# A two-layer attention kernel on one core: query tiles scaled one by one, copies moved to VectorE, and a few steps of the first attention moved

## The chip, the cores and the metric

The kernel runs on one core of a Trainium2 chip, in one launch. The metric is the device time of the launch in microseconds (us). The engines are PE (TensorE's matmuls), PEld (its weight loads, which overlap the matmuls), DVE (VectorE), ACT (ScalarE), POOL (GpSimd) and SP (SyncE, which issues DMAs). All data are float32.

## The reference, cut to what matters

Eight sequences of 256 tokens with 256 features go through two layers. Each layer is a cross-attention to a context of 192 features, followed by a feed-forward block; both have a residual sum.

```
x = x + attention0(layernorm(x), ctx)      # 16 heads of 16
x = x + soft_moe(x)                        # 8 experts, 128 slots each per sample, hidden 1024
x = x + attention1(layernorm(x), ctx)      # 16 heads of 64, with an output bias
x = x + channel_mix(layernorm(x))

attention:  q = x Wq, k = ctx Wk, v = ctx Wv, split into heads
            out = softmax(q k^T * head_dim**-0.5) v Wo      # the first with a key mask
soft_moe:   logits of tokens against slots (both normalised)
            combine = softmax over slots, dispatch = softmax over tokens
            slots = dispatch^T x -> two-layer expert with gelu -> combine
```

The soft mixture of experts works on groups of two sequences here, so its routing needs, for each group, a softmax over slots for each token and a softmax over tokens for each slot.

## The kernel before, in words

**Stages.** Four stages follow one another: the first attention (0 to about 259 us of the profiled span), the mixture of experts (259 to 895), the second attention (895 to 1269) and the channel mix (1269 to the end). The routing of the first group of the mixture of experts is laid into the last steps of the first attention, so that PE has work there.

**Order.** `matmul` and `transpose` (L74, L77) keep PE's instructions in the order in which the program issues them. `vec` and `gps` do the same for VectorE and GpSimd while `Ordered.held` is set, which it is through the loop of the first attention (L103 is the line of their instructions). Elsewhere a scheduler may reorder the other engines' instructions. Semaphore waits come out of the data: an instruction waits for whatever wrote what it reads, and for whatever still reads what it overwrites.

**PSUM.** Three kinds of buffer are used: "big" (128x1024, two banks, 2 buffers), "mm" (128x512, one bank, 3 buffers, `ps_mm`) and "o" (128x512, one bank, 1 buffer, `ps_o`). A "mm" buffer is taken in turn by every projection, transpose and logit piece, so its third successor waits until its reader is done.

**First attention.** The loop at L907 runs over steps `h` of about 3 us; eight steps serve one sequence. A step issues eight score matmuls for queries and eight for the exponentials' side (`scores`, ACT's exponentials are `ex` at L585), then whatever `whole[h]` lists: small pieces put there by `at(h, piece)`. A piece may return a function, its second half, which is called in the next step, after that step's scores. Pieces that the change touches are:

- `normed0(b)` (L680): the layer-normed input of sequence `b`, `xh`, written by GpSimd for the later sequences.
- `values0(b)` (L708 and L709): V of a sequence, in two halves. The first half issues two matmuls and returns the second, which issues the others and copies V out of PSUM.
- `slot_scaled(e2)` and `slot_piece(e2)` (L412): the slot embeddings of two experts are scaled by GpSimd (`sn`), transposed by PE (`pt_sn`) and scaled out of PSUM by two VectorE instructions into `snT`.
- `values(b, t2, to)`: the attention's product with V for half of the heads of a sequence (PE `o <- ex,V`), its transposes and division, ten steps after the scores. It returns `turn_back`, a VectorE transpose for the next step. `turn_back` is called ahead of the halves, in one step behind them.
- `routing0(b)`: the routing of one sequence of the first group. Its pieces are N (`scale`), P (`prepare`), T (`by_token`, logits `ln`), S (`by_slot`, the transposed logits `ls`, with their maxima, exponentials and sums), U (`turn_token`, PE's `ptn` transposes, copied into `CT`), D (`turn_slot`, PE's `pts` transposes, copied into `dt`, which is the buffer `wq` in the profile) and F (`fill`, PE's `pf`, the slots). They are laid out by hand in two strings at L891: a letter, the step, and the piece's arguments.

**Second attention.** After a prologue for the first sequence, the tick loop at L1605 runs over ticks `n` of about 10.3 us, four to a sequence, each with two pairs of heads. In program order a tick has: the values of tick n-3 (`values`, PE's `o`, then its copy `ot` at L1414), one query piece for the next sequence (`q_piece`, L1296), the projection of tick n-4 (only for the last tick of a sequence, PE's `po`), the transposes of tick n-2 (`transposes`, PE's `pe`, copied into `et` at L1395 by VectorE and ACT in turn), the normalisation of tick n-1 (GpSimd), one piece of keys or values of a later sequence, and the scores of tick n (PE's `sc`, VectorE's maxima `nm` at L1361, ACT's exponentials `ex` at L1366).

A query piece covers two tiles of 128 query features by 256 tokens. Both lie in one "mm" buffer, that is in one bank:

```
pq = ps_mm(f"q1_{b}_{t2}").rearrange("p (t n) -> p t n", t=2)
for i in range(2):          # two tiles, two matmuls each
    ...matmul(pq[:, i, :], ...)
nc.vector.tensor_scalar(
    to["QT"][:, 2 * t2 : 2 * t2 + 2, :], pq, HD1**-0.5, None, ALU.mult
)
```

There are 32 query pieces, four in the prologue and 28 in ticks. In three of four ticks the transposes come straight after the query piece on PE; in the fourth the projection lies between.

Of the kernel before, what the change touches and what calls it, by code (L numbers as in the profile page):

```python
# [12 lines left out]
ALU = mybir.AluOpType  # L13
# [3 lines left out]
B, S, D, C = 8, 256, 256, 192  # L17
NT = B * S // P
H = 16
HD0, HD1 = 16, 64  # L20
# [43 lines left out]
def kernel(ctx: ExitStack, tc: tile.TileContext, a: dict, out: bass.AP):  # L64
    nc = tc.nc
# [42 lines left out]
    vec, gps = Ordered(nc.vector), Ordered(nc.gpsimd)  # L108
# [175 lines left out]
    with ExitStack() as l0:  # L284
# [126 lines left out]

        def slot_piece(e2):  # L412
            pt = transposed(sns[e2], f"sn_{e2}", transpose)
            for c in range(2):
                vec.tensor_scalar(
                    snT[:, c, e2 * 256 : (e2 + 1) * 256],
                    pt[:, c, :],
                    sgam[:, c : c + 1],
                    None,
                    ALU.mult,  # L420
                )

# [10 lines left out]
        tos = []  # L435
# [228 lines left out]
        def at(h, f):  # L664
            whole.setdefault(h, []).append(f)
# [9 lines left out]
        for p, when in ((1, (1, 2, 2, 3, 3)), (2, (5, 7, 8, 9, 11)), (3, (17, 19, 21, 23, 27))):  # L675
            parts, got = ln_parts(p, f"l0_{2 * p}")
            stats0 += [got] * 2
            for h, part in zip(when, parts):
                at(h, part)
        for b, h in ((2, 4), (3, 6), (4, 15), (5, 23), (6, 31), (7, 39)):  # L680
            at(h, lambda b=b: normed0(b))
        at(0, lambda: keys0(0, 1))
        at(1, lambda: queries0(0, 1))
# [12 lines left out]
        for p in range(1, 4):  # L696
            h, b = 16 * (p - 1), 2 * p
            if h:
                at(h, lambda b=b: tokens0(b))
                at(h + 3, lambda p=p: key_rows(p))  # L700
                at(h + 4, lambda p=p: keys0(p, 0))
                at(h + 5, lambda b=b: queries0(b, 0))
                at(h + 7, lambda b=b: queries0(b, 1))
                at(h + 8, lambda b=b: tokens0(b + 1))
                at(h + 12, lambda p=p: keys0(p, 1))
            at(h + 13, lambda b=b: queries0(b + 1, 0))
            at(h + 15, lambda b=b: queries0(b + 1, 1))
            at(h + 17, lambda b=b: values0(b))  # L708
            at(h + 25, lambda b=b: values0(b + 1))  # L709

        for e in range(E):
            at(7 + e, lambda e=e: slot_sum(e))
        at(19, slot_scale)
        for e2 in range(4):
            at((23, 31, 39, 43)[e2], lambda e2=e2: slot_scaled(e2))
            at((25, 33, 41, 45)[e2], lambda e2=e2: slot_piece(e2))
        for g, when in enumerate(((29, 31, 37, 39), (47, 49, 53, 61), (61, 64, 65, 66))):
            for i, h in enumerate(when):
                at(h, lambda g=g, i=i: moe_mean(g, [i]))
# [21 lines left out]
        def routing0(b):  # L741
# [58 lines left out]
            def turn_token(t):  # L800
                for m in range(2):
                    pt = ps_mm(f"ptn_{b}_{t}_{m}")
                    for i in range(4):
                        e = 4 * m + i
                        transpose(
                            pt[:, i * P : (i + 1) * P], st[f"en{t}"][:, e * P : (e + 1) * P]
                        )
                    (vec.tensor_copy if m else nc.scalar.copy)(
                        set0["CT"][:, b, 4 * m : 4 * m + 4, t * P : (t + 1) * P],
                        pt.rearrange("p (e n) -> p e n", e=4),  # L810
                    )
# [48 lines left out]
            def turn_slot(q):  # L860
                for t in range(2):
                    pt = ps_mm(f"pts_{b}_{q}_{t}")
                    for i in range(4):
                        transpose(
                            pt[:, i * P : (i + 1) * P],
                            st[f"es{q}"][:, i, t * P : (t + 1) * P],
                        )
                    (vec.tensor_copy if b and t else nc.scalar.copy)(dt[:, t, :], pt)

            def fill(q, c):  # L870
                pf = ps_mm(f"pf_{b}_{q}_{c}")
# [18 lines left out]
        for b, plan in enumerate(  # L890
            (  # L891
                "N43 P47 T48.00 T49.10 S50.00 S51.01 T52.01 T53.11 D54.0 U55.0 U55.1 F56.00 F57.01 "
                "S58.10 S59.11 D62.1 F63.10 F65.11",
                "N55 P60 T61.00 T64.10 S65.00 S66.01 T67.01 T68.11 D69.0 U69.0 S70.10 S70.11 U70.1 "
                "F71.00 F72.01 D73.1 F73.10 F74.11",
            )
        ):
            does = dict(zip("NPTUSDF", routing0(b)))
            for step in plan.split():
                when, _, args = step[1:].partition(".")  # L900
                at(int(when), lambda f=does[step[0]], args=args: f(*map(int, args)))
# [4 lines left out]
        for h in range(8 * B + 12):  # L906
            q, k = [  # L907
                (i // 8, i % 8 // 2, i % 2) if 0 <= i < 8 * B else None for i in (h, h - 6)
            ]
            if q or k:  # L910
                scores(q, k)

            late = turn_back if h == 8 * B + 7 else None
            if turn_back and not late:
                turn_back()
            later = [g for g in [f() for f in halves] if g]
            if late:
                late()
            turn_back = None
            k = h - 4  # L920
            if k % 4 == 0 and 0 <= k < 8 * B:
                pair_maxima(k // 8, k % 8 // 4, tos[k // 8])
            halves = later + [g for g in [f() for f in whole.get(h, ())] if g]
            k = h - 10
            if k % 4 == 0 and 0 <= k < 8 * B:
                turn_back = values(k // 8, k % 8 // 4, tos[k // 8])
        Ordered.held = False

# [272 lines left out]
    with ExitStack() as l1:  # L1201
# [61 lines left out]
        def proj1(b):  # L1263

            to = {}

            def normed_piece():
                mv, rstd = xat_stats[b // 2]  # L1270
                to["xh"] = normed(b, mv, rstd, "l1", of=4)

            def xt_piece():
                pt = transposed(to["xh"], f"x1_{b}", transpose)
                to["xT"] = p1.tile([P, 2, S], F32, tag="xT", bufs=1, name=f"xT1_{b}")
                nc.vector.tensor_copy(to["xT"], pt)  # L1276
                for t in range(2):
                    nc.gpsimd.tensor_tensor(
                        x_sb[:, 2 * b + t, :], x_sb[:, 2 * b + t, :], bo, ALU.add
                    )  # L1280

            def q_piece(t2):
                if t2 == 0:
                    to["QT"] = p1.tile([P, 8, S], F32, tag="QT", bufs=2, name=f"QT1_{b}")
                pq = ps_mm(f"q1_{b}_{t2}").rearrange("p (t n) -> p t n", t=2)
                for i in range(2):
                    t = 2 * t2 + i
                    for c in range(2):
                        matmul(
                            pq[:, i, :],  # L1290
                            lhsT=wq[:, c, t * P : (t + 1) * P],
                            rhs=to["xT"][:, c, :],
                            start=(c == 0),
                            stop=(c == 1),
                        )
                nc.vector.tensor_scalar(  # L1296
                    to["QT"][:, 2 * t2 : 2 * t2 + 2, :], pq, HD1**-0.5, None, ALU.mult
                )

            def values_of(u):  # L1300

                if u == 0:
                    to["V"] = p1.tile([P, 2, DA], F32, tag="V", bufs=2, name=f"V1_{b}")
                pv = [ps_mm(f"v1_{b}_{u}_{h}") for h in range(2)]
                t0 = S * b + u * P
                cols = [slice(h * 512, (h + 1) * 512) for h in range(2)]
                for h in range(2):
                    matmul(
                        pv[h],
                        lhsT=ctx0T[:, t0 : t0 + P],  # L1310
                        rhs=wv[:, 0, cols[h]],
                        start=True,
                        stop=False,
                    )

                def halves():
                    for h in range(2):
                        r = slice(64 * h, 64 * h + 64)
                        matmul(
                            pv[h],  # L1320
                            lhsT=ctx1T[r, t0 : t0 + P],
                            rhs=wv[r, 1, cols[h]],
                            start=False,
                            stop=True,
                        )
                    nc.scalar.copy(to["V"][:, u, cols[0]], pv[0])
                    nc.vector.tensor_copy(to["V"][:, u, cols[1]], pv[1])

                return halves

            return (
                to,
                [lambda t=t: q_piece(t) for t in range(4)],
                [lambda u=u: values_of(u) for u in range(2)],
                normed_piece,
                xt_piece,
            )

        def steps1(b, to):
# [4 lines left out]
            for t in range(8):  # L1344
# [53 lines left out]
                def values(t=t, tag=tag, st=st):  # L1398
# [12 lines left out]
                                stop=(c == 1),  # L1411
                            )
                    if t % 2 == 1:
                        nc.scalar.copy(blk["ot"][:, t - 1 : t + 1, :], blk["o"])  # L1414

                def project(tag=tag):
                    po = ps_mm(f"po_{tag}").rearrange("p (q d) -> p q d", q=2)
# [288 lines left out]
```

## Time and profile before

| what | value |
| --- | --- |
| time, median of 3 runs | 1332.44 us (1332.26 to 1334.61) |
| the profiled execution | 1334.6 us, its span 1332.8 us |
| mean granted TensorE clock | 0.997 |
| PE busy | 1315.3 us, 99% of the span |
| VectorE busy | 567.7 us, 43% |
| ACT busy | 576.6 us, 43% |
| GpSimd busy | 245.1 us, 18% |

Times in the profile are of one execution. A float32 matmul is recorded as two matmuls, so that a query piece of four matmuls shows eight. A line of the timeline gives the start, the time from the first start to the last end of what is grouped in it, the engine, the line, the operation with its output and inputs, the tile sizes and the number of instructions; the bracket gives the idle time of the engine before it and what ended that. A row of the windows gives, for a stretch of the span, its length, the busy time (and the number of instructions) of PE, PEld, DVE, ACT and POOL, the granted clock of TensorE as a share of full speed, the share of the DMA engines and GB/s. A row of the groups gives the busy time and the mean duration in ns, then the idle time of the engine before the group and what ended it.

### The profile page before, as it was taken

What the parts mean: (1) busy time and instruction counts of PE and PEld (TensorE: products, weight loads), DVE (VectorE), ACT (ScalarE), POOL (GpSimd) and SP (SyncE); (2) the same over time, 40 slices, a digit from 0 to 9 for tenths busy, and PEclk for the clock granted to TensorE, in tenths of its full rate; (3) what the DMA queues carried; (4) which work ended last, traced back from release to release, by engine and by line L of the source; (5) the groups of instructions that cost most, each with busy time, mean ns of one, the idle gap of its engine ahead of it and who ended that gap; (6) DMA issues with size and microseconds to landing.
All of it is one profiled execution on the core that took longest, in us unless ns stands there. A gap on an engine that the chain in (4) does not pass through costs nothing.

```text
span 1332.8 us, 19111 instructions
## 1 busy us (share of the span) xinstructions
PE 1315.3 (99%) x7520; PEld 955.6 (72%) x7520; DVE 567.7 (43%) x1131; ACT 576.6 (43%) x1396; POOL 245.1 (18%) x285
## 2 busy tenths in 40 slices
PE   9999999999999999999999999999999999999998
PEld 5666655577778786788867888866676676677777
DVE  6677777433320233322333110024544544544675
ACT  2644455353522363423634122213545445445653
POOL 3222412200000010100101000012323323333423
PEclk9999999899999999999999999999999999999999
DMA  7100000134134232342323434350000000000001
GB/s 218 65 1 2 1 1 1 63 103 134 68 134 134 70 132 78 124 134 72 130 82 120 134 118 151 103 154 1 0 1 1 1 1 1 1 1 1 1 8 56
DMA packets 59145, 86.85 MB, mean 65 GB/s; under 512 B 3376, under 2 KB 49072, under 8 KB 59056
## 3 DMA queue, kind: packets, MB, share of 16 engines
q1 hardware_dynamic: 58480, 85.11, 19.5%
q8 instruction: 59, 0.97, 0.3%
q10 hardware_dynamic: 576, 0.52, 0.1%
q14 instruction: 30, 0.25, 0.1%
HBM read 83.53 MB, written 2.10 MB: 64 GB/s over the span
## 4 chain that ended last, share of the span: by engine, by line
PE 94%; ACT 4%; DVE 2%; issue 0%; POOL 0%; ACTq 0%; DVEq 0%; POOLq 0%
PE ph L1104 17%; PE pe L1120 16%; PE sc L74 9%; PE q L74 7%; PE o L74 7%; PE po L74 5%; PE k L74 5%; PE pe L77 4%; PE v L74 4%; PE pc L1146 4%; PE pf L1050 3%; PE ln L968 3%; PE pf L74 1%; PE pk L74 1%; PE pr L74 1%; PE ln L74 1%
## 5 line engine op out<-in xcount | busy, mean ns | idle before, releaser
L1112 ACT ACTIVATE ht<-ph,b 128x256 f32<-128x256 f32 x256 | 119.3, 474 | 371.6 <-PE ph L1104 371.2
L1104 PE MATMUL ph<-slots,w 128*128 128x256 f32 x1024 | 266.9, 384 | 0.9 <-ACT ht L1112 0.2
L1120 PE MATMUL pe<-w,ht 128*128 128x256 f32 x1024 | 263.3, 381 | 0.0
L1104 PEld LDWEIGHTS ph<-slots,w 128*128 128x128 f32 x1024 | 182.3, 189 | 54.0 <-ACT ht L1112 21.7
L1120 PEld LDWEIGHTS pe<-w,ht 128*128 128x128 f32 x1024 | 192.0, 190 | 29.9 <-DVE slots L1129 4.2
L1379 POOL TENSOR_TENSOR ex<-ex,rz 128x1024 f32<-128x1024 f32 x64 | 119.9, 1895 | 229.9 <-DVE rz L1377 222.4
L1366 ACT ACTIVATE ex<-sc,nm 128x256 f32<-128x256 f32 x256 | 117.4, 484 | 53.0 <-DVE nm L1361 53.0
L585 ACT ACTIVATE ex<-sc 128x512 f32<-128x512 f32 x128 | 75.1, 598 | 68.7 <-PE sc L74 64.9
L74 PE MATMUL sc<-KT,QT 17*128 17x256 f32 (+1 forms) x1024 | 103.5, 380 | 0.8 <-ACT QT L520 0.7
L1028 POOL TENSOR_TENSOR es<-es,zs 128x1024 f32<-128x1024 f32 x12 | 22.7, 1894 | 432.8 <-DVE zs L1027 432.8
L103 DVE TENSOR_REDUCE NM<-sc 128x2 f32<-128x512 f32 x128 | 87.6, 691 | 32.7 <-PE sc L74 27.6
L1129 DVE TENSOR_TENSOR slots<-pe,b 128x512 f32<-128x512 f32 x32 | 22.1, 692 | 185.1 <-PE pe L1120 185.1
L74 PE MATMUL q<-xT,wq 128*128 128x256 f32 x384 | 94.9, 391 | 0.9 <-DVE xT L1276 0.9
L74 PEld LDWEIGHTS sc<-KT,QT 17*128 17x128 f32 (+1 forms) x1024 | 75.9, 186 | 20.8 <-issue 11.6
L74 PEld LDWEIGHTS q<-xT,wq 128*128 128x128 f32 x384 | 69.2, 189 | 28.1 <-issue 14.4
L1361 DVE TENSOR_REDUCE nm<-sc 128x4 f32<-128x1024 f32 x64 | 75.4, 1219 | 7.7 <-PE sc L74 4.7
L74 PE MATMUL po<-wo,ot 128*128 128x256 f32 x320 | 72.5, 382 | 0.0
L77 PE MATMUL pe<-ident,ex 128*128 128x128 f32 x512 | 70.2, 278 | 0.8 <-DVE et L1395 0.7
L74 PEld LDWEIGHTS po<-wo,ot 128*128 128x128 f32 x320 | 60.1, 190 | 10.9 <-issue 3.2
L77 PEld LDWEIGHTS pe<-ident,ex 128*128 128x128 f32 x512 | 56.5, 140 | 15.3 <-issue 7.6
L1395 ACT COPY et<-pe 128x512 f32<-128x512 f32 x64 | 37.5, 599 | 63.9 <-PE pe L77 63.4
L74 PE MATMUL o<-et,V 128*64 128x256 f32 x512 | 62.8, 385 | 0.8 <-ACT ot L1414 0.8
(227 smaller groups left out, 1665.9 us busy)
## 6 DMA issues: line engine op xcount, KB each, us to landing
w<-in_w_dram SPq DMA_DIRECT2D x64, 1024.0 KB, 5.7
b<-in_b_dram SPq DMA_DIRECT2D x32, 128.0 KB, 6.8
x_sb<-in_x_dram SPq DMA_DIRECT2D x3, 512.0 KB, 7.0
ctx0T<-in_ctxT_dram SPq DMA_DIRECT2D x4, 256.0 KB, 8.6
ctx1T<-in_ctxT_dram SPq DMA_DIRECT2D x8, 128.0 KB, 8.0
se<-in_slots_dram SPq DMA_DIRECT2D x1, 1024.0 KB, 11.1
wq<-in_wq_dram SPq DMA_DIRECT2D x1, 1024.0 KB, 5.1
wo<-in_wo_dram SPq DMA_DIRECT2D x1, 1024.0 KB, 12.1
```

The lines of the kernel that those rows point to most:

```text
L74: tc.keep_in_program_order(nc.tensor.matmul(out, lhsT=lhsT, rhs=rhs, start=start, stop=stop))
L77: tc.keep_in_program_order(nc.tensor.transpose(out, in_, ident))
L103: ins = op(*args, **kwargs)
L585: nc.scalar.activation(ex[:, 2 - 2 * i : 4 - 2 * i, :], sc[1 - i][:, :, 1, :], AF.Exp)
L968: nc.tensor.matmul(pl[:, m * 512 : (m + 1) * 512], lhsT=st["xnT"][:, c, t * P : (t + 1) * P], rhs=snT[:, c, m * 512 : (m + 1) * 512], star ...
L1104: nc.tensor.matmul(ph, lhsT=c_["w1"][:, c, hc * P : (hc + 1) * P], rhs=slots[e][:, c * 256 : (c + 1) * 256], start=(c == 0), stop=(c == 1),)
L1112: nc.scalar.activation(ht, ph, AF.Gelu, bias=b1[:, e, hc : hc + 1])
L1120: nc.tensor.matmul(c_["pe"][:, b, :], lhsT=c_["ht"][hc][:, b * SL : (b + 1) * SL], rhs=c_["w2"][:, hc, :], start=(hc == 0), stop=(hc == HI ...
L1146: nc.tensor.matmul(pc[:, :D], lhsT=CT[:, bl, e, t * P : (t + 1) * P], rhs=eos[e][:, bl, :], start=(e == 0), stop=(e == E - 1),)
L1361: nc.vector.tensor_reduce(nm, sc, AX.X, ALU.max, negate=True)
L1366: nc.scalar.activation(ex[:, i, qb, :], sc[:, i, qb, :], AF.Exp, bias=nm[:, i, qb : qb + 1], accum_out=z[:, i, qb : qb + 1],)
L1379: nc.gpsimd.tensor_tensor(ex, ex, rz.rearrange("p h q -> p (h q)").unsqueeze(2).to_broadcast([P, 4, S]), ALU.mult,)
```

## The change

It has seven parts.

1. `slot_piece` returns its two VectorE scalings as a second half, and runs at steps 24, 32, 40 and 45 (25, 33, 41 and 45 before).
2. `normed0` of sequences 5, 6 and 7 runs at steps 19, 27 and 35 (23, 31 and 39 before).
3. `values0` of sequences 2 to 5 issues both halves in one step. Sequences 6 and 7, and 0 and 1, which are laid out elsewhere, keep two steps.
4. In the second sequence's routing, the copy of the first `ptn` into `CT` and both copies of the first `turn_slot` are made by VectorE instead of ACT.
5. In the second plan, the piece U70.1 becomes U71.1, and the last `values` is issued one step later, at h = 71, after the halves and ahead of that step's pieces. `turn_back` is called ahead of the halves in every step.
6. `q_piece` scales each of its two query tiles after that tile's matmuls (128x256), instead of both at the end (128x512).
7. `values` of the second attention copies `ot` by VectorE instead of ACT.

```diff
         def slot_piece(e2):
             pt = transposed(sns[e2], f"sn_{e2}", transpose)
-            for c in range(2):
-                vec.tensor_scalar(
...
+            def scaled():
+                for c in range(2):
+                    vec.tensor_scalar(
...
+            return scaled
...
-        for b, h in ((2, 4), (3, 6), (4, 15), (5, 23), (6, 31), (7, 39)):
+        for b, h in ((2, 4), (3, 6), (4, 15), (5, 19), (6, 27), (7, 35)):
             at(h, lambda b=b: normed0(b))
...
-            at(h + 17, lambda b=b: values0(b))
-            at(h + 25, lambda b=b: values0(b + 1))
+            for i in range(2):
+                at(
+                    h + 8 * i + 17,
+                    lambda b=b + i: values0(b) if b > 5 else values0(b)(),
+                )
...
-            at((25, 33, 41, 45)[e2], lambda e2=e2: slot_piece(e2))
+            at((24, 32, 40, 45)[e2], lambda e2=e2: slot_piece(e2))
...
-                    (vec.tensor_copy if m else nc.scalar.copy)(
+                    (vec.tensor_copy if m or (b and t == 0) else nc.scalar.copy)(
                         set0["CT"][:, b, 4 * m : 4 * m + 4, t * P : (t + 1) * P],
...
-                    (vec.tensor_copy if b and t else nc.scalar.copy)(dt[:, t, :], pt)
+                    on_vec = b and (t or q == 0)
+                    (vec.tensor_copy if on_vec else nc.scalar.copy)(dt[:, t, :], pt)
...
-                "N55 P60 T61.00 T64.10 S65.00 S66.01 T67.01 T68.11 D69.0 U69.0 S70.10 S70.11 U70.1 "
-                "F71.00 F72.01 D73.1 F73.10 F74.11",
+                "N55 P60 T61.00 T64.10 S65.00 S66.01 T67.01 T68.11 D69.0 U69.0 S70.10 S70.11 "
+                "U71.1 F71.00 F72.01 D73.1 F73.10 F74.11",
...
-            late = turn_back if h == 8 * B + 7 else None
-            if turn_back and not late:
+            if turn_back:
                 turn_back()
+                turn_back = None
             later = [g for g in [f() for f in halves] if g]
-            if late:
-                late()
-            turn_back = None
             k = h - 4
...
+            k = 8 * B - 4
+            if h == k + 11:
+                turn_back = values(k // 8, k % 8 // 4, tos[k // 8])
             halves = later + [g for g in [f() for f in whole.get(h, ())] if g]
             k = h - 10
-            if k % 4 == 0 and 0 <= k < 8 * B:
+            if k % 4 == 0 and 0 <= k < 8 * B - 4:
                 turn_back = values(k // 8, k % 8 // 4, tos[k // 8])
...
-                nc.vector.tensor_scalar(
-                    to["QT"][:, 2 * t2 : 2 * t2 + 2, :], pq, HD1**-0.5, None, ALU.mult
-                )
+                    nc.vector.tensor_scalar(
+                        to["QT"][:, t, :], pq[:, i, :], HD1**-0.5, None, ALU.mult
+                    )
...
-                        nc.scalar.copy(blk["ot"][:, t - 1 : t + 1, :], blk["o"])
+                        nc.vector.tensor_copy(blk["ot"][:, t - 1 : t + 1, :], blk["o"])
```

More of the change, by code (lines that the diff above doesn't have):

```diff
@@ L413, in slot_piece @@
             pt = transposed(sns[e2], f"sn_{e2}", transpose)
-            for c in range(2):
-                vec.tensor_scalar(
[L416 to L420, printed above, removed]
-                )
+            def scaled():
+                for c in range(2):
+                    vec.tensor_scalar(
+                        snT[:, c, e2 * 256 : (e2 + 1) * 256],
+                        pt[:, c, :],
+                        sgam[:, c : c + 1],
+                        None,
+                        ALU.mult,
+                    )
+            return scaled
         Vs = [w0.tile([P, 2, H, 32], F32, name=f"V0_{i}") for i in range(2)]
@@ L1295, in q_piece @@
                         )
-                nc.vector.tensor_scalar(
-                    to["QT"][:, 2 * t2 : 2 * t2 + 2, :], pq, HD1**-0.5, None, ALU.mult
-                )
+                    nc.vector.tensor_scalar(
+                        to["QT"][:, t, :], pq[:, i, :], HD1**-0.5, None, ALU.mult
+                    )
             def values_of(u):
```

## The prediction

> **What bounds the kernel now.** First the page: the busy line, and the engine shares of the chain that ended last.
>
> ```profile
> PE 1315.3 (99%) x7520; PEld 955.6 (72%) x7520; DVE 567.7 (43%) x1131; ACT 576.6 (43%) x1396; POOL 245.1 (18%) x285
> ...
> PE 94%; ACT 4%; DVE 2%; issue 0%; POOL 0%; ACTq 0%; DVEq 0%; POOLq 0%
> ```
>
> PE is busy for 99% of the span, and no other engine for half of it. Work taken off ACT or VectorE gains nothing by itself; only a wait of PE, or a new one, moves the end. The windows by stage give the second attention:
>
> ```profile
> 895.00:1269.00 374.00, 372.08 (x2228) 254.60 (x2228) 182.97 (x302) 186.92 (x633) 124.53 (x82) 1.00 0.00 1
> ```
>
> Here PE (first pair) idles 1.92 us of 374. The waits of PE (total, times, longest) are all there is to win:
>
> ```profile
> PE sc L74 <- ACT ex L585: 3.4, 8, 0.7
> ...
> PE ls L77 <- ACT wq L868: 1.5, 1, 1.5
> PE ptn L77 <- ACT CT L808: 1.1, 2, 0.7
> PE q L74 <- DVE xT L1276: 0.9, 1, 0.9
> PE v L74 <- ACT et L1395: 0.8, 1, 0.8
> PE o L74 <- ACT ot L1414: 0.8, 1, 0.8
> PE pe L77 <- DVE et L1395: 0.7, 1, 0.7
> ...
> PE ph L1104 <- ACT ht L1112: 0.2, 1, 0.2
> ```
>
> QT's scaling (L1296) appears nowhere: PE never waits for it now. The timeline of one tick of the second attention:
>
> ```profile
> 1066.55 1.99 PE L74 MATMUL q<-xT,wq 128*128 128x256 f32 x8
> ...
> 1068.38 2.20 PE L77 MATMUL pe<-ident,ex 128*128 128x128 f32 x16
> ...
> 1068.58 0.69 DVE L1296 TENSOR_SCALAR QT<-q 128x512 f32<-128x512 f32 x1 [1.75 <-PE q L74]
> 1068.86 0.62 ACT L1414 COPY ot<-o 128x512 f32<-128x512 f32 x1
> ```
>
> Four query matmuls (two records each) run through while VectorE idles, then the transposes follow at once. One scaling reads both tiles of one bank after the last matmul.
>
> The execution profiled took 1334.6 us (span 1332.8, 1.8 around it), 2.2 over the median of 1332.44; sums start from 1334.6.
>
> **(a) Query tiles scaled one by one, 32 pieces.** It adds 32 VectorE instructions, which alone would hide. But the third query matmul writes the bank that the first scaling reads, and in the changed kernel's instruction stream it carries a wait for that scaling; PE's in-order queue (transposes, values, scores) stands behind it. The trace of before has no such wait in this stage; its nearest is PE ph <- ACT ht (0.2), where two tiles also share a bank and matmuls of another line hide the rest. Here nothing stands between the two tiles. Step by step: at 1066.55 the first record has a pitch of 0.32, the others 0.216, so the fourth starts at 1067.30 and ends at 1067.68, and the fifth, without a wait, would start at 1067.52: 0.16 lost. VectorE starts 0.04 after a matmul's end (1068.54 to 1068.58). For 128x256 out of PSUM, the groups by form:
>
> ```profile
> L1296 DVE TENSOR_SCALAR QT<-q 128x512 f32<-128x512 f32 x32 | 22.1, 692 | 57.3 <-PE q L74 57.3
> ...
> L103 DVE TENSOR_SCALAR snT<-pt_sn,sgam 128x256 f32<-128x256 f32 x8 | 3.5, 479 | 1.1 <-PE pt_sn L77 0.8
> ```
>
> So 0.48. PE resumes 0.055 after (xT ends 912.297, q starts 912.352), and the first record after a wait has the 0.32 pitch: 0.10 more. 0.16+0.04+0.48+0.055+0.10 = 0.84 us, x32 = **+26.9**. Bounds: without the longer pitch 0.73; with a slower release (0.146, read at a transposes' bank release) and a slower restart 1.06: +23.4 to +34. A gain is excluded, since the matmul can start no earlier than now.
>
> The Trainium skill, "PSUM — Partial Sum Buffer", section on bank collisions, speaks against this edit: an engine's read and TensorE's write in one bank and quadrant must not overlap, though they are at different addresses. By it, too, the wait can't be ordered away.
>
> **(b) VectorE not free at the first tile.** In the first two ticks its nm reduction runs until 920.39 and 926.81, while the fourth record ends at 919.91 and 926.34; one tick near 1166 has a root in the way: 2 x 0.36 + 0.3 = **+1.0** (0 to 1.5).
>
> **(c) What the split gives back.** In 20 ticks the transposes follow q; the ninth record starts 0.19 late there, waiting for the scaling to leave one of the three banks. After the split the last scaling is 0.21 shorter. I take 0.15 x 20 = **-3.0** (-5 to 0). In the other ticks the projection stands there: nothing.
>
> **(d)** PE v <- ACT et (0.8, tick at 930) sits behind the first stalls and vanishes into them (0.8); PE q <- DVE xT shrinks by 0.2, since xT's copy starts at 911.62 right behind the prologue's last scaling, now 0.21 shorter: **-1.0** (-1.5 to 0).
>
> **(e) ot copied by VectorE, 32 copies.** ACT loses 620 ns each, which it needs nowhere; VectorE gains 0.69 each (its 128x512 COPY et<-pe). Queued behind it: the first scaling. At 1066.6 o ends, VectorE is free at 1066.83, so ot lasts until 1067.52; the first tile is ready at 1067.72. It fits by 0.2. In the last two ticks nothing else hides it (+0.2 each), and at the end A0's copy and et stand 0.6 behind it twice, against 0.5 saved of PE o <- ACT ot: 0.4 + 1.2 - 0.5 = **+1.1** (-0.5 to +2.5).
>
> **(f) First attention, loop.** The waits PE sc <- ACT ex at 90.29, 115.55 and 140.79 (0.39 and like) get the slot transposes (0.53 of PE work) moved in front: 3 x 0.5 saved. The second half of a batch's values (0.63) moves ahead of the wait of 0.31 at 67.25: 0.35. The other sc waits (35, 41, 64, 192, 210) have nothing put into them. On POOL, xh moved to step 19 runs before krows at 75.57 and is done by 75.2; sn is ready at 88.4, before its transposes at 89.75. The V copies move ahead of ex by one step, with 0.1 to spare on ACT. None of the moved steps issues a DMA, so SP's queue is passed by nothing. **-1.9** (-3 to +1).
>
> **(g) End of the first attention.** PE ls waits 1.46 for ACT's wq copy, queued behind exponentials, and ptn 0.68 for ACT's CT copy; both copies go to VectorE, and the last values move between. Windows (PE's busy time in the first pair, the granted clock in the last but two):
>
> ```profile
> 237.92:241.34 3.42, 1.83 (x13) 1.12 (x12) 1.94 (x6) 3.42 (x9) 0.00 (x0) 1.00 0.00 0
> 241.34:244.75 3.41, 2.73 (x13) 2.33 (x13) 1.38 (x2) 1.08 (x3) 0.00 (x0) 0.50 0.00 0
> ...
> 910.35:913.76 3.41, 2.46 (x14) 1.95 (x14) 1.93 (x4) 0.00 (x0) 1.06 (x2) 1.00 0.00 0
> ```
>
> A window with PE busy for 1.83 of 3.42 is followed by half clock until 248.16; one with 2.46 of 3.41 isn't. Replayed with copies of 0.69 on VectorE: ls at 239.68 and 240.29, o 240.73 to 242.6, ptn to 243.5, first fill 243.9 after a wait of 0.4, second fill at 248.65 where it now is at 253.82: **-5.1**, since PE is then busy for some 74% and the clock holds; if it still falls, -2.2 (the waits alone). I take the first, by the window at 910. The two shorter runs of before may lack this half-clock stretch; after would be the same either way.
>
> The Trainium skill, "TensorE: Matmul & The Clock Gate", section "Why this matters for your kernels", asks for no PE gap above about 3 us; the trace lost half its clock behind a gap of 1.46. By the page's rule the clock would not depend on these waits and the sum would be 2.9 longer. The same page's section on a second failure mode lets frequent short idles between groups make the clock swing, which 32 stalls would invite: as an estimate, a half-clock window per loop piece is 28 x 1.7 = 48 more. The window at 910, shorter of work than a tick with one stall (2.57 of 3.41 at worst), held 1.00.
>
> **Sum.** 1334.6 + 26.9 + 1.0 - 3.0 - 1.0 + 1.1 - 1.9 - 5.1 = **1352.6**.
>
> **Rivals.** *The second tile's matmuls don't wait in effect* (faster than before). Without (a) and (b) the sum is 1324.7. Below 0.24 us per piece it beats the median of before (7.7/32), below 0.16 by over 0.2%. For it: VectorE is idle 1.75 us ahead of the scaling. Against: the wait stands in the stream, and the scaling alone is 0.48 long. 0.05; another 0.02 for a cost between 0.16 and 0.32, no change.
>
> *VectorE becomes the bound.* If the ot copy, or the et copies behind it, doesn't fit the 0.2 us in the 32 ticks, each first scaling is late by 0.1 to 0.2: 1356 to 1359. For it: that slack is the smallest in the tick. Against: VectorE idles before et too (0.21). 0.10.
>
> *The clock falls.* It stays half at the end of the first attention (1355.5), or falls in the prologue, where four query pieces follow each other with PE busy about 70%: one window at half clock is 1.7, two are 3.4, to 1358. For it: 2.46 of 3.41 is the only row of that kind. 0.10.
>
> The forecast: 0.73. The change can also do what it says with (c) larger; that is in the range.
>
> **How the numbers follow.** (a) alone spans +23.4 to +34, and the others, not all at one end, some 3 either way. 1345.5 to 1358.5 takes in the forecast's low end (0.73 per piece, 1349, less 3.5) and most of the two slower rivals; left out are the faster side, the far end of (a), and the rivals combined. 0.2%, about what a measurement of this kernel can tell from no change, is 2.7 us. Faster 0.05, same 0.02, slower 0.93.
>
> **What would show it.** In the waits of PE after, a line PE q <- DVE QT with some 32 times and 0.55 to 0.7 each (0.04 + 0.48 + 0.055; the rest of the 0.84 is lost pitch); stage 895 to 1269 longer by about 24; PE ls <- ACT wq gone, and no 0.50 clock near 245. Wrong, if q's records keep their 0.216 pitch through all eight, if that line is under 8 us in all, or if clocks below 1.00 appear inside the second attention's ticks.

## The result, and the profile after

The changed kernel takes 1350.39 us (median of 4 runs, 1350.12 to 1350.59) against 1332.35 (1331.90 to 1334.61): a ratio of 1.0132, 95% interval 1.0114 to 1.0149. The forecast was 1352.6. The execution profiled took 1350.21, its span 1348.4.

The page after, busy line and chain. PE has 1.9 us more of busy time and 15.6 more of span, so what was added is waiting; VectorE's share of the chain goes from 2% to 4%:

```profile
PE 1317.2 (98%) x7520; PEld 951.3 (71%) x7520; DVE 595.1 (44%) x1197; ACT 560.5 (42%) x1362; POOL 244.6 (18%) x285
...
PE 93%; DVE 4%; ACT 3%; issue 1%; DMA 0%; SPq 0%; ACTq 0%; DVEq 0%
```

PE's waits after (total, times, longest). The first line is new, once for each query piece; `ls <- wq` and the long wait of `ptn` are gone, and `sc <- ex` is down from 8 to 4; `pe <- ex` and `pt_xf <- et` are new, at the end of the second attention:

```profile
PE q L74 <- DVE QT L1307: 17.4, 32, 0.9
PE sc L74 <- ACT ex L590: 1.9, 4, 0.7
...
PE pt_xf L77 <- DVE et L1406: 0.9, 1, 0.9
PE pe L77 <- POOL ex L1390: 0.8, 1, 0.8
PE q L74 <- DVE xT L1287: 0.8, 1, 0.8
...
PE pe L77 <- DVE et L1406: 0.6, 1, 0.6
PE ptn L77 <- ACT CT L817: 0.4, 1, 0.4
```

The timeline of the tick that the prediction showed, now in the changed kernel, PE's part and then VectorE's:

```profile
1071.92 1.13 PE L74 MATMUL q<-xT,wq 128*128 128x256 f32 x4
1073.57 1.13 PE L74 MATMUL q<-xT,wq 128*128 128x256 f32 x4 [0.52 <-DVE QT L1307]
1074.54 2.04 PE L77 MATMUL pe<-ident,ex 128*128 128x128 f32 x16
```

```profile
1072.12 0.66 DVE L1425 COPY ot<-o 128x512 f32<-128x512 f32 x1
1073.09 0.42 DVE L1307 TENSOR_SCALAR QT<-q 128x256 f32<-128x256 f32 x1 [0.31 <-PE q L74]
1074.74 0.42 DVE L1307 TENSOR_SCALAR QT<-q 128x256 f32<-128x256 f32 x1 [1.22 <-PE q L74]
```

The eight records of a query piece are now two groups of four, with a wait between them that ends when the first scaling does. The copy of `ot` ends 0.3 us before the first tile is ready, so it isn't what is waited for.

Between the same landmarks of PE, the times in us of the two profiled executions, and of kernels that share the code of a stretch (e2 has the first attention of before; e5 has the second attention of before):

| stretch | before | after | same code as before, other execution |
| --- | --- | --- | --- |
| first exponentials of the first attention to the first `ph` | 225.16 | 217.99 | 222.25 (e2) |
| first `ph` to the prologue's first `q` | 644.71 | 645.06 | 644.64 (e2) |
| prologue's first `q` to the last query piece | 315.16 | 335.95 | 315.16 (e5) |
| last query piece to the end of the last `po` | 65.90 | 67.44 | 65.89 (e5) |
| from there to the end | 47.95 | 47.96 | 47.96 (e5) |

The second attention loses 20.8 + 1.5; the first gains 7.2 against the profiled execution of before, and 4.3 against an undisturbed execution of the same code.

### The profile page after: what moved, and what is told of

Same layout as the page of the kernel before. It is cut to its first block, busy times and chain, and to the rows that moved or that the text cites. A ratio compares the mean times of both kernels' runs of the same rounds, so it can differ in the third digit from the quotient of the medians.

```text
span 1348.4 us, 19137 instructions
## 1 busy us (share of the span) xinstructions
PE 1317.2 (98%) x7520; PEld 951.3 (71%) x7520; DVE 595.1 (44%) x1197; ACT 560.5 (42%) x1362; POOL 244.6 (18%) x285
## 4 chain that ended last, share of the span: by engine, by line
PE 93%; DVE 4%; ACT 3%; issue 1%; DMA 0%; SPq 0%; ACTq 0%; DVEq 0%
PE ph L1115 17%; PE pe L1131 16%; PE sc L74 9%; PE q L74 7%; PE o L74 6%; PE po L74 5%; PE k L74 5%; PE pe L77 4%; PE v L74 4%; PE pc L1157 4%; PE pf L1061 3%; PE ln L979 3%; PE pf L74 1%; DVE QT L1307 1%; PE pk L74 1%; PE pr L74 1%
## 5 line engine op out<-in xcount | busy, mean ns | idle before, releaser
L74 PE MATMUL q<-xT,wq 128*128 128x256 f32 x384 | 103.5, 400 | 18.1 <-DVE QT L1307 17.4
L77 PE MATMUL pe<-ident,ex 128*128 128x128 f32 x512 | 67.0, 277 | 1.4 <-POOL ex L1390 0.8
```

Source lines behind the costliest of these rows:

```text
L74: tc.keep_in_program_order(nc.tensor.matmul(out, lhsT=lhsT, rhs=rhs, start=start, stop=stop))
L77: tc.keep_in_program_order(nc.tensor.transpose(out, in_, ident))
```

## Experiments

All times are medians; ratios are to the kernel before, run on the same chip, with the 95% interval.

**e1: the whole scaling back, all other parts kept.**

```diff
-                    nc.vector.tensor_scalar(
-                        to["QT"][:, t, :], pq[:, i, :], HD1**-0.5, None, ALU.mult
-                    )
+                nc.vector.tensor_scalar(
+                    to["QT"][:, 2 * t2 : 2 * t2 + 2, :], pq, HD1**-0.5, None, ALU.mult
+                )
```

> The changed kernel, with the query pieces scaled whole again (128x512, one instruction after four matmuls); all other parts stay. Theory (the third query matmul waits for the first scaling, since both tiles lie in one bank): the 32 waits go, 32 x 0.78 + 0.8, the 20 x 0.16 given back to the transposes goes too, and the wait of v for et (0.9) comes back: 1350.4 - 25.9 + 3.2 + 0.9 = 1328.6. Rival (VectorE's 27 us of added work is what the time pays): only 32 x 0.155 = 5 of it goes, 1345.

1329.31, ratio 0.9979 (0.9970 to 0.9987): the theory to within 0.7. The changed kernel without this one part is faster than the kernel before, though VectorE keeps the 22 us of `ot` copies.

**e2: the split alone, on the kernel before** (the reverse of the diff above).

> The kernel before, with the query pieces scaled tile by tile and nothing else. Theory: 1332.4 + 25.9 - 3.2 - 0.9 = 1354.2. Rival (VectorE's work): 1332.4 + 5 = 1337. A third reading (the split stalls only because ot's copy was moved to VectorE beside it): near 1332.

1354.79, ratio 1.0167 (1.0154 to 1.0181). The split stalls in the same way with `ot` on ACT, so the move of `ot` has no share in it. From the first `q` to the last query piece it takes 335.86, after 335.95.

**e3: each query tile in a bank of its own.**

```diff
-                pq = ps_mm(f"q1_{b}_{t2}").rearrange("p (t n) -> p t n", t=2)
                 for i in range(2):
                     t = 2 * t2 + i
+                    pq = ps_mm(f"q1_{b}_{t}")[:, 0:S]
...
```

> The changed kernel, with each query tile in a PSUM buffer (bank) of its own; 64 scalings of 128x256 as in the changed kernel, and one more buffer taken from the three in each piece. Theory: no wait of q for QT, and the bank still comes free early for the transposes: 1350.4 - 25.9 + 0.9 = 1325.4. Rival (VectorE's work): it does the same work, 1350. Third reading: the additional buffer makes the transposes or the values wait for a reader instead, 0.2 to 0.6 per piece: 1332 to 1345.

1325.30, ratio 0.9947 (0.9933 to 0.9960). Its 64 scalings are those of the changed kernel; only the PSUM buffer, and with it the bank, is another for each tile, and 25 us go. Every buffer here fills whole banks, so the runs don't separate two tiles in one buffer from two tiles in one bank. PE's timeline of one tick shows the piece in one run again, and the transposes 0.16 shorter than before's 2.20:

```profile
1048.80 1.99 PE L74 MATMUL q<-xT,wq 128*128 128x256 f32 x8
1050.63 2.04 PE L77 MATMUL pe<-ident,ex 128*128 128x128 f32 x16
```

The stretch of query pieces takes 311.96, 3.2 less than before: that is what the split gives back (c), with no stall to pay for it.

**e4: the first tile ahead of the values, still one bank.**

```diff
...
+            if b < B:
+                projs[b][1][i](0)
             stage(3, n - 3)
             if b < B:
-                projs[b][1][i]()
+                projs[b][1][i](1)
```

> The changed kernel, with the first query tile of each tick issued ahead of the values of the tick (16 matmul records, 1.95 us) and the second tile behind them; the two tiles still share a bank. Theory: the wait of about 0.57 for the first scaling ends while the values run, in the 25 ticks that have values; the four pieces of the prologue and the first three ticks keep it: 7 x 0.78 + 0.7 = 6.2 left of 25.9: 1350.4 - 19.7 + 0.5 = 1331. Rival (VectorE's work): 1350.

`(0)` is the first tile's matmuls and scaling, `(1)` the second's. 1336.03, ratio 1.0028 (1.0016 to 1.0039), 5 more than the theory. The first wait line below has the 7 pieces that were to keep it and no others, so the cover works; the timeline of a tick then shows no wait, but the order itself costs:

```profile
PE q L74 <- DVE QT L1309: 4.3, 7, 0.9
```

```profile
1053.10 1.13 PE L74 MATMUL q<-xT,wq 128*128 128x256 f32 x4
1054.16 1.95 PE L74 MATMUL o<-et,V 128*64 128x256 f32 x16
1056.03 1.13 PE L74 MATMUL q<-xT,wq 128*128 128x256 f32 x4
```

Single records: the pitch (from a record's start to the next one's) is 0.309 at the last `q` ahead of `o` and 0.320 at the first `q` behind it, where inside a piece it is 0.216. One more change from `q` (weights 128x128) to `o` (128x64) and back costs 0.093 + 0.104 = 0.197 us; in 25 ticks that is 4.9, about the whole miss. From `q` to the transposes, whose weights are 128x128 too, the pitch stays at 0.216.

**e9: both tiles first, then two scalings, one bank.**

```diff
+                for i in range(2):
                     nc.vector.tensor_scalar(
-                        to["QT"][:, t, :], pq[:, i, :], HD1**-0.5, None, ALU.mult
+                        to["QT"][:, 2 * t2 + i, :], pq[:, i, :], HD1**-0.5, None, ALU.mult
                     )
```

> The changed kernel with both query tiles' matmuls first and then the two scalings of 128x256, tiles in one bank: the same 64 instructions, but no wait between the matmuls. Theory (it is the wait between the tiles that costs, not the number of instructions): e1's 1329.3, plus 0.16 in the 20 ticks where the third group of transposes waits for the bank, since two scalings take 0.85 where one takes 0.69: 1332.5. Rival (the number of VectorE instructions costs): 1350.

1332.71, ratio 1.0004 (0.9996 to 1.0013). The same number and size of VectorE instructions as the changed kernel, and 17.7 us less: not the work on VectorE, but the wait between the tiles. It is behind e1 by 3.4, since the transposes now find the bank later: their group takes 2.42, against 2.20 before, in each of 20 ticks.

```profile
1062.00 1.99 PE L74 MATMUL q<-xT,wq 128*128 128x256 f32 x8
...
1063.83 2.42 PE L77 MATMUL pe<-ident,ex 128*128 128x128 f32 x16
```

**e10: each tile scaled in two halves.**

```diff
-                    nc.vector.tensor_scalar(
-                        to["QT"][:, t, :], pq[:, i, :], HD1**-0.5, None, ALU.mult
-                    )
+                    for z in range(2):
+                        nc.vector.tensor_scalar(
+                            to["QT"][:, t, z * P : (z + 1) * P],
+                            pq[:, i, z * P : (z + 1) * P],
+                            HD1**-0.5,
+                            None,
+                            ALU.mult,
+                        )
```

> The changed kernel with each query tile's scaling done in two instructions of 128x128: the third matmul waits for both. Theory (the wait is as long as VectorE's reads of the first tile): two of about 0.29 instead of one of 0.425, 32 x 0.155 = 5 more, 1355.4. Rival (a wait has a fixed price, whatever is waited for): 1350.4.

1352.12, ratio 1.0150 (1.0136 to 1.0164): 1.7 above the changed kernel, not 5. The timeline of a tick gives the reason:

```profile
1073.75 0.49 DVE L1308 TENSOR_SCALAR QT<-q 128x128 f32<-128x128 f32 x2 [0.31 <-PE q L74]
...
1074.30 1.13 PE L74 MATMUL q<-xT,wq 128*128 128x256 f32 x4 [0.58 <-DVE QT L1308]
```

Two scalings of 0.29 overlap and take 0.49 together, 0.065 more than the single 0.425; PE's wait is 0.06 longer (0.58 against 0.52), and 32 x 0.064 = 2.0 (the stretch of query pieces is 1.9 longer). So the wait does follow the reads; the expectation had added up two durations that overlap.

**e5: the first attention's parts alone** (e1 with the copy of `ot` back on ACT).

```diff
-                        nc.vector.tensor_copy(blk["ot"][:, t - 1 : t + 1, :], blk["o"])
+                        nc.scalar.copy(blk["ot"][:, t - 1 : t + 1, :], blk["o"])
```

> The changed kernel with the whole second attention as before (query pieces scaled whole, ot copied by ACT), so the parts in the first attention alone. It is e1 with the copy of ot back on ACT. Theory: the copy on VectorE costs some 0.7 at the end and in two ticks: 1329.3 - 0.7 = 1328.6; against before, the first attention's 1.8 (loop) and 2.2 (end) are left: 1328.3. Rival (the copy on VectorE frees ACT and pays): 1330 to 1331.

1328.16, ratio 0.9965 (0.9953 to 0.9978). Against e1, the copy on VectorE costs 1.15; in the trace of e1, 0.8 without its stretch at half clock (behind the last query piece it takes 68.30, and e9 and e3, with the same copy and no such stretch, 66.65).

**e3b: own banks, `ot` on ACT** (e3 with the same edit).

> e3 (each query tile in a bank of its own) with the copy of ot back on ACT. Theory: 1325.3 - 0.7 = 1324.6. Rival (VectorE is where ot belongs): 1326 to 1327.

1325.51, ratio 0.9945 (0.9932 to 0.9957): the same as e3. In the trace it gains the 0.76 at the end and loses 0.23 in the ticks; the rest lies within the scatter of the runs. With banks of their own, where `ot` is copied doesn't matter.

**e6: only the copies at the end of the first attention to VectorE.**

```diff
-                    (vec.tensor_copy if m else nc.scalar.copy)(
+                    (vec.tensor_copy if m or (b and t == 0) else nc.scalar.copy)(
...
-                    (vec.tensor_copy if b and t else nc.scalar.copy)(dt[:, t, :], pt)
+                    (vec.tensor_copy if b and (t or q == 0) else nc.scalar.copy)(dt[:, t, :], pt)
```

> The kernel before, with only the copies of CT and dt at the end of the first attention moved to VectorE; values and U70.1 stay in place. Theory: the waits of ls (1.46) and ptn (0.68) for ACT go, up to 0.4 turns into a wait for exponentials: 1332.3 - 1.8 = 1330.5. Rival (the order of the last values is what fills the wait): within 0.5 of 1332.3.

1330.73, ratio 0.9987 (0.9978 to 0.9996). The wait of `ls` is gone; that of `ptn` stays:

```profile
241.65 0.66 PE L77 MATMUL ptn<-ident,krows 128*128 128x128 f32 x4 [0.68 <-ACT CT L808]
```

**e7: only the order at the end of the first attention** (last values at h = 71, U71.1, `turn_back` first).

```diff
-S70.11 U70.1 F71.00
+S70.11 U71.1 F71.00
...
+            k = 8 * B - 4
+            if h == k + 11:
+                turn_back = values(k // 8, k % 8 // 4, tos[k // 8])
...
```

> The kernel before, with only the moves at the end of the first attention (last values one step later, U71.1, turn_back ahead of the halves); the copies stay on ACT. Theory: ls still waits 1.46 for ACT's copy, the wait of ptn (0.68) goes, since the values stand between: 1332.2 - 0.7 = 1331.5. Rival (without the copies on VectorE the moves do nothing): within 0.3 of 1332.2. With e6 (-1.5) the parts should add up to the end's 2.2.

1331.15, ratio 0.9992 (0.9983 to 1.0001). The reverse of e6: `ls` waits 1.5, the 0.68 of `ptn` is gone. From the first exponentials to the first `ph`, e6 takes 220.84, e7 221.11 and both with the loop's gain 217.99, against 222.25 (e2): 1.4 + 1.1, about the 2.4 that both have together.

**e8: only the moves in the loop of the first attention, and e8s: of these only `slot_piece` and `normed0`.**

```diff
...
-            at((25, 33, 41, 45)[e2], lambda e2=e2: slot_piece(e2))
+            at((24, 32, 40, 45)[e2], lambda e2=e2: slot_piece(e2))
...
-        for b, h in ((2, 4), (3, 6), (4, 15), (5, 23), (6, 31), (7, 39)):
+        for b, h in ((2, 4), (3, 6), (4, 15), (5, 19), (6, 27), (7, 35)):
...
-            at(h + 17, lambda b=b: values0(b))          # e8 only
-            at(h + 25, lambda b=b: values0(b + 1))
+            for i in range(2):
+                at(h + 8 * i + 17, lambda b=b + i: values0(b) if b > 5 else values0(b)())
```

> The kernel before, with only the moves in the loop of the first attention (slot pieces, normed0, values0). Theory: 1.8 less, as between the two traces: 1330.4. Rival (what the loop gains early, the end waits off again): 1332.

> As e8, without the change of values0: slot pieces and normed0 alone. Theory: the slot transposes fill three waits of 0.39 and 0.35 for values0 is missing: 1330.4 + 0.35 = 1330.8. Rival (the gain is that of values0, whose V copies get ahead of the exponentials): 1332.

e8 1330.16, ratio 0.9983 (0.9974 to 0.9992); e8s 1332.35, ratio 1.0003 (0.9994 to 1.0012): the slot pieces alone give nothing. PE's timeline of e8s and then of e8, at the place where before waits 0.39 at 90.29:

```profile
90.07 0.60 PE L77 MATMUL pt_sn<-ident,sn 128*128 128x128 f32 x4
90.62 0.82 PE L74 MATMUL sc<-QT,KT 18*128 18x256 f32 x8
...
93.18 0.88 PE L74 MATMUL sc<-QT,KT 18*128 18x256 f32 x8 [0.24 <-ACT ex L589]
```

```profile
92.03 0.70 PE L74 MATMUL v<-wv,ctx1T 64*128 64x256 f32 x4
92.66 0.71 PE L74 MATMUL sc<-QT,KT 18*128 18x256 f32 x8
```

In e8s the transposes fill the wait at step 25, and step 25, now without them, is too short: step 26 waits 0.24 for exponentials, and its first scores take 0.88 instead of the 0.71 that e8 shows. In e8 the second half of the values stands in that gap. Step by step, e8 is ahead by 0.42 from step 19, 0.91 from 27, 1.39 from 35 and 1.87 from 43; e8s is ahead by 0.14 at the start of steps 26, 34 and 42 and has lost it again one step later; it keeps no more than 0.02.

## Why the prediction was right, point by point

**(a) The wait between the tiles: right, at 0.784 instead of 0.84.** In the trace after, in 29 of the 32 pieces, the fourth record's start lies 0.895 to 0.898 ahead of the fifth's, where the pitch was 0.216, and the fifth then has a pitch of 0.320: 0.896 - 0.216 + 0.104 = 0.784. VectorE starts 0.037 after the fourth record and PE 0.055 after the scaling, as taken. The miss is in the scaling: 0.425, not 0.48. For the same reason the wait itself is 0.52 in these pieces, below the 0.55 to 0.7 that was to show it. The groups by form after:

```profile
L1307 DVE TENSOR_SCALAR QT<-q 128x256 f32<-128x256 f32 x64 | 27.2, 424 | 49.6 <-PE q L74 49.6
```

The row taken for it, snT, has the same shape but a factor for each partition where QT has a constant; that this makes the difference wasn't tried. 32 x 0.784 = 25.1 instead of 26.9. e3 shows that the place which the tiles share in PSUM is the cause, e9 that the number of instructions isn't.

**(b)** 0.35 twice and 0.10 near 1175: 0.8 instead of 1.0. **(c)** 0.16 in each of the 20 ticks, -3.2 instead of -3.0, and e3 has it without the stall. The 0.19 that the prediction reads is 0.165 in the trace of before (0.274 from the eighth record's start to the ninth's, 0.109 after), so 0.15 was a good choice from a wrong reading. **(d)** The wait of v for et is gone and xT's is 0.17 shorter: -1.0, as forecast.

**(e)** +0.8 instead of +1.1: 0.76 behind the last query piece (e9 66.65 against e5 65.89, where both have the wait-free pieces) and 0.03 before it (e1 315.19 against e5 315.16). It is about what the waits at the end make up: `pt_xf <- et` 0.9 and `pe <- ex` 0.8 are new where VectorE copies `ot`, and 0.8 of `o <- ot` is gone. The copy fits between o's end and the first tile in every tick, so the rival that it becomes the bound is out.

**(f) The sum right (-1.87 for -1.9), its parts wrong.** Three fills of 0.5 by the slot transposes and one of 0.35 by values had been added up. e8s shows that the slot transposes gain nothing alone: the step of the working that failed is that it asked which wait the moved work fills, and not what the step that it leaves does without it. That the sum came out is luck. The four gains of 0.42 to 0.48 come with the values' second half; in three of them the slot piece has to go ahead too, by the traces, since before waits in front of step 25 and not behind it. Values in one step without the slot pieces wasn't run.

**(g) The waits right, the clock not.** The copies and the order take away both waits, as replayed; against the profile of before the stretch up to the first `ph` is 7.17 shorter, 1.87 of it the loop's, so 5.3 for the forecast 5.1. But 2.9 of it was the half clock of that one execution (225.16 against e2's 222.25). The prediction took the half clock for what a window with 1.83 us of work in 3.42 brings. In all 14 traces the granted clock changes only at whole multiples of 3.413 us from its first record, so the windows of another execution have to be laid on that execution's own grid. On it, e8, whose end of the first attention is that of before with the same waits of 1.46 and 0.68:

```profile
238.10:241.51 3.41, 1.61 (x13) 1.37 (x14) 2.01 (x5) 2.28 (x6) 0.00 (x0) 1.00 0.00 0
241.51:244.92 3.41, 3.41 (x39) 1.84 (x40) 1.56 (x3) 1.71 (x8) 0.00 (x0) 1.00 0.01 2
```

Less work in the window, and the clock stays at 1.00. The same at the end of the second attention, where e1 (the first two rows) and e4 (the last two) have windows with equal work, and only e1 loses the clock behind it:

```profile
1265.65:1269.06 3.41, 1.70 (x14) 1.23 (x13) 3.41 (x6) 1.17 (x2) 1.22 (x1) 1.00 0.00 0
1269.06:1272.48 3.42, 3.42 (x16) 1.96 (x17) 3.24 (x9) 1.71 (x4) 0.00 (x0) 0.50 0.00 0
```

```profile
1272.19:1275.60 3.41, 1.70 (x15) 1.23 (x13) 3.41 (x6) 1.17 (x2) 1.32 (x1) 1.00 0.00 0
1275.60:1279.01 3.41, 3.41 (x27) 2.37 (x28) 3.41 (x10) 1.71 (x4) 0.00 (x0) 1.00 0.00 0
```

So PE's busy time in one window doesn't decide it by itself; what does stays open. Against the usual execution the end gains 2.4, near the 2.2 that was kept as the second value. The misreading hardly shows in the total, since the sum started from the same execution: 1334.6 - 5.1 is 1329.5, and 1332.35 - 2.4 is 1330.0. The prediction had said that the shorter runs of before may lack the half clock, and they mostly do: of 16 runs of before beside e1 to e4, three lie between 1334.4 and 1334.9, with a mean clock of 0.997, and the others between 1331.2 and 1332.6, with 1.00. e2 has two of each kind (1355.9 and 1356.3; 1352.8 and 1353.7), so its median lies between them.

**The sum with measured sizes**, from the median of before: 1332.35 + 25.1 + 0.8 - 3.2 - 1.0 + 0.8 - 1.9 - 2.4 = 1350.6, and 0.4 for a stretch that no step named: from the first `ph` on, every kernel that has e6's copies takes 0.35 to 0.4 longer up to the second attention, in two places of the mixture of experts (near 480 and 573) where the order of instructions is the same. Why isn't settled. 1351.0 against 1350.39 measured; starts of the profiled executions differ by up to 1.2.

**The rule on the clock.** By the section of the Trainium skill that was weighed, "TensorE: Matmul & The Clock Gate", "Why this matters for your kernels", which asks for no PE gap above about 3 us, gaps of this length shouldn't cost the clock. In the profile of before and in that of e1 half clock followed on gaps of at most 1.46 and 0.90; in e8 and e4 it did not. The page's other warning, of a clock that swings under frequent short idles, isn't borne out here: with 32 waits of 0.52 and more, the granted clock of the whole execution after is 1.0.

**Rivals.** That the second tile doesn't wait in effect is excluded by the first wait line. That the clock stays half at the end of the first attention or falls in the prologue: it did neither, in the prologue with 11.63 busy of 15 us.

## What to carry to other kernels

In this kernel two tiles in one PSUM buffer of one bank act as one: the instruction that reads the first tile stops PE before it may write the second. Splitting the read paid when each tile had a buffer and a bank of its own (1325.3 and 1325.5, the best of all). Other work between the tiles hides the wait as well, but that it pays wasn't shown: in e4 the changes of matmul shape that came with it cost more than the split gave back. When work is moved into a wait, look at the step that it leaves; the wait may just move there. A duration of a stage in one profile can hold a disturbance that belongs to that execution alone: compare it with a second kernel that shares the code before a gain is counted.

## What the runs showed of the hardware

The granted clock changed only at whole multiples of 3.413 us from its first record (before: 69, 71 and 389). At the end of the first attention it fell to 0.50 behind a window with 1.83 us of work in before and stayed at 1.00 behind one with 1.61 in e8; at the end of the second it fell in e1 and stayed in e4, both behind 1.70. Two VectorE instructions in a row out of PSUM overlap in their records: 0.49 for two of 0.29 in e10, and 0.76 for two of 0.42 in e9. A change from matmuls with weights of 128x128 to ones of 128x64 and back cost PE 0.197 us in e4 (pitches of 0.309 and 0.320 for 0.216).
